# Storing the last group's expert results by tile and gathering them by token, with eight fours merged into the last attention

## Chip, core and metric

The kernel runs on one core of one Trainium2 chip. The metric is device time in microseconds (us) of one execution. Five engines work beside each other: PE (matrix multiplication), DVE (vector), ACT (scalar), POOL (GpSimd) and SP, which here only issues transfers. SP and ACT issue transfers with fixed addresses. POOL issues the indirect ones, whose row numbers stand in a tile. All transfers run on the same 16 DMA engines.

## What is computed

One decoder layer in float32 over 8 batches of 512 tokens and 256 features: a rolling attention, a cross attention with a causal mask, and a mixture of 16 routed experts, of which each token takes the best two, beside two shared ones.

```python
x = x + attn(layernorm(x), W_A, W_V, W_O, b_O)
x = x + xattn(layernorm(x), ctx, ctx, WK, WV, WQ)
flat = layernorm(x)
out = einsum(silu(flat @ wg_s) * (flat @ wu_s), wd_s)          # shared experts
probs = softmax(flat @ router_w)
weights, indices = top_k(probs, 2)                             # two experts a token
h = silu(flat @ wg_r[e]) * (flat @ wu_r[e]) * comb[e]
x = x + out + einsum(h, wd_r)                                  # routed experts
```

## The kernel before

The batches are worked one after another. Batch b runs its attentions while the next batch's first part and the last batch's shared experts are merged in, in an order written out by hand (`ORDER`, `ORDER6`, `ORDER7`). A framework (Tile) then takes the instructions, places the waits, hands out the buffers, and orders each engine's queue by a planner with its own estimates of durations. Within its queue an engine works strictly in order. A tile's tag names a small set of buffers (`bufs`); a new tile of that tag waits until everything that read an old one is done.

**Routed experts.** The batches form two groups (`GROUPS`): batches 0 to 6, and batch 7 alone. `ranked` (L567 on) counts for each token where it stands in the list of each of its two experts. `send` (L606) then writes the normalised row, with the token's number and weight, to that place in the DRAM tensor `xg` of the group, by one indirect transfer for 128 rows. `tiled` (L661 on) works out how the 16 lists fall into tiles of 128 rows: `begin` is the first tile of an expert, `n` its count of rows. The first group has 72 tiles, the second 24. Four tiles make a "four" (`QT = 4`), so there are 18 and 6 fours.

For each four `fetch` (L736) loads the rows, `pick` (L745, L755) the weights of the experts, `turn` (L763 to L776) transposes the rows, `hidden` (L790 to L794) and `down` (L805 to L819) compute, and `put` (L827) writes each of the four result tiles to the DRAM tensor `yg` by token: an indirect transfer on POOL whose row numbers (`to`) come with the rows. Rows that fill up a tile have a number beyond the bound, and are dropped. The result tiles `y` lie in buffers of the tag `y` (eight tiles, two fours) or `xT` (four buffers of one four each, which other tiles use too: the normalised rows `x2T` of batch 7 hold one of them until the shared experts of batch 7 are done).

**The end.** `MIXED` is the number of the first group's fours that are merged step by step into the last attention; the fours from there on are merged with the ranking, the sending and the tiling of batch 7 (`sorting`). The six fours of the second group follow, merged with the shared experts of batch 7 (`late`, L632 to L651). `take` (L879) loads what was put for one batch, two times 512 KB, on SP; `join` (L890) adds both to `x` on DVE, and L892 stores the batch. The takes of a batch use one of three pairs of buffers, by the batch's number modulo 3: `qT` for batches 0, 3 and 6, `v2` for 1, 4 and 7, `row` for 2 and 5. A take of the first group waits for all 72 puts of that group; the take of batch 7 for all 24 of its own.

Of the kernel before, what the change touches and what calls it, by code (L numbers as in the profile page):

```python
# [16 lines left out]
P = 128  # L17
B, S, D = 8, 512, 256
NT = S // P
KC = D // P  # L20
H, HD = 16, 16
NE = 16
# [4 lines left out]

GROUPS = ((0, 1, 2, 3, 4, 5, 6), (7,))

MIXED = 5  # L30

STAY = (4, 5, 6, 7)

# [2 lines left out]
QT = 4  # L36


def n_tiles(g):

    n = (len(GROUPS[g]) * S * 2 + NE * (P - 1)) // P
    return -(-n // QT) * QT
# [43 lines left out]
def decoder_layer(ctx: ExitStack, tc: tile.TileContext, x, ctxT, waT, wvT, woT, bo, wkT, xwv, wqT, wr, wg, wu, wd, out):  # L86
    nc = tc.nc

    const = ctx.enter_context(tc.tile_pool(name="const", bufs=1))
    sb = ctx.enter_context(tc.tile_pool(name="sb", bufs=2))  # L90
# [4 lines left out]
    st = [dict() for _ in range(B)]  # L95
# [99 lines left out]
    grp = []  # L195
    for g, bs in enumerate(GROUPS):
        n = len(bs) * S
        first = const.tile([P, NE], F32, name=f"first{g}")
        nc.vector.tensor_scalar(first, expert_no, float(n + P), float(P), ALU.mult, ALU.add)


        xg = dram.tile([NE * (n + P) + P, XW], F32, tag=f"xg{g}", bufs=1, name=f"xg{g}")
        grp.append({
            "g": g, "n": n, "first": first, "xg": xg,
            "yg": dram.tile([2 * n, D], F32, tag=f"yg{g}", bufs=1, name=f"yg{g}"),
        })


# [189 lines left out]
    def steps_back(b):  # L398
# [168 lines left out]
        def ranked():  # L567

            g, bi = where[b]
            G = grp[g]  # L570
            tt, red = nc.vector.tensor_tensor, nc.vector.tensor_reduce
            both = small.tile([P, NT, NE], F32, tag="both", bufs=1, name=f"both{b}")
            tt(both, s["oh"][0], s["oh"][1], ALU.add)
            pk = ps.tile([P, 2, NT, NE], F32, tag="tr", bufs=2, name=f"pk{b}")
            nc.tensor.matmul(pk[:, 0], before, both, start=True, stop=True)
            nc.tensor.matmul(pk[:, 1], ones, both, start=True, stop=True)
            run = small.tile([P, NT + 1, NE], F32, tag="run", bufs=2, name=f"run{b}")
            nc.vector.tensor_copy(run[:, 0], G["first"] if bi == 0 else G["run"][:, NT])
            for c in range(NT):
                tt(run[:, c + 1], run[:, c], pk[:, 1, c], ALU.add)  # L580
            G["run"] = run
            at = small.tile([P, NT, NE], F32, tag="at", bufs=1, name=f"at{b}")
            tt(at, pk[:, 0], run[:, :NT], ALU.add)
            place = small.tile([P, 2, NT], I32, tag="place", bufs=2, name=f"place{b}")
            for r in range(2):
                hit = small.tile([P, NT, NE], F32, tag="hit", bufs=2, name=f"hit{b}_{r}")
                tt(hit, s["oh"][r], at, ALU.mult)
                spot = small.tile([P, NT], F32, tag="spot", bufs=2, name=f"spot{b}_{r}")
                red(spot, hit, AX.X, ALU.add)
                behind = nc.vector.tensor_copy(place[:, r], spot).ins  # L590
                with tc.issue_after(behind):
                    nc.vector.tensor_scalar_add(s["row"][r][:, :, 0], tok[:, bi * NT:(bi + 1) * NT], float(r * G["n"]))
            s["place"] = place
# [67 lines left out]
    def tiled(g):  # L661

        G = grp[g]
        T = n_tiles(g)
        tt = nc.vector.tensor_tensor

        def new(n, shape=(P, NE), dt=F32):
            return small.tile(list(shape), dt, tag=n, bufs=1, name=f"{n}_{g}")

        def per_tile(n, of, dt=F32):  # L670
            w, out = new("held"), new(n, (P, 1), dt)
            tt(w, here, of, ALU.mult)
# [24 lines left out]
        fit = new("fit")  # L697
        nc.vector.scalar_tensor_tensor(fit, G["run"][:, NT], -float(P), row, ALU.add, ALU.min)
        last = new("last", (P, 1))
        nc.vector.tensor_reduce(last, here, AX.X, ALU.add)  # L700
        nc.vector.tensor_scalar(last, last, -float(NE * (G["n"] + P)), float(NE * (G["n"] + P)), ALU.mult, ALU.add)
        row0 = per_tile("row0", fit)
        tt(row0, row0, last, ALU.add)
        G["table"] = row0, ex

        tt(row, row, fit, ALU.subtract)
        G["had"] = per_tile("had", row)

    def tabled(g):

# [15 lines left out]
    def steps_routed(g):  # L726
# [32 lines left out]
        def turn(q):  # L759
            def f():  # L760
                xs = G["xs", q]
                G["to", q] = small.tile([P, QT], I32, tag="to", bufs=8, name=f"to{g}_{q}")
                nc.vector.tensor_tensor(G["to", q], xs[:, :, 0], G["far"][:, q * QT:(q + 1) * QT], ALU.max)  # L763

                G["w", q] = small.tile([P, QT], F32, tag="w", bufs=8, name=f"w{g}_{q}")
                nc.vector.tensor_copy(G["w", q], xs[:, :, 1])
                xT = sb.tile([P, KC, QT, P], F32, tag="xsT", name=f"xsT{g}_{q}")
                for k in range(KC):
                    pt = ps.tile([P, 512], F32, tag="tr", bufs=2, name=f"pxt{g}_{q}_{k}")
                    for i in range(QT):  # L770
                        nc.tensor.transpose(pt[:, i * P:(i + 1) * P], xs[:, i, 2 + k * P:2 + (k + 1) * P], ident)  # L771
                    to = xT[:, k].rearrange("p i t -> p (i t)")
                    if k == 0:
                        nc.scalar.copy(to, pt)
                    else:
                        nc.vector.tensor_copy(to, pt)  # L776
                G["xT", q] = xT
            return f
# [19 lines left out]
        def down(q):  # L798
            def f():
                h, wdn = G["h", q], G["wdn", q]  # L800
                tag = "mm" if g or q >= MIXED else "gu"
                py = [ps.tile([P, QT // 2, D], F32, tag=tag, bufs=3, name=f"py{g}_{q}_{o}") for o in range(2)]
                for j in range(QT // 2):
                    for o in range(2):
                        nc.tensor.matmul(py[o][:, j, :], h[o * MR:(o + 1) * MR, j, :], wdn[o * MR:(o + 1) * MR, j, :], start=True, stop=True)  # L805
                if g == 0 and (q < MIXED or q % 2 == 0):
                    y = [sb.tile([P, D], F32, tag="y", bufs=8, name=f"y{g}_{q}_{i}") for i in range(QT)]
                else:

                    y = sb.tile([P, QT, D], F32, tag="xT", bufs=4, name=f"y{g}_{q}")  # L810
                    y = [y[:, i, :] for i in range(QT)]
                for o in range(2):
                    for j in range(QT // 2):
                        i = 2 * j + o
                        w = G["w", q][:, i:i + 1]
                        if j == 0:
                            nc.scalar.mul(y[i], py[o][:, j, :], w)  # L817
                        else:
                            nc.vector.tensor_scalar_mul(y[i], py[o][:, j, :], w)  # L819
                G["y", q] = y  # L820
            return f

        def put(q, n):
            def f():
                o, j = divmod(n, 2)
                i = 2 * j + o
                ins = nc.gpsimd.indirect_dma_start(  # L827
# [9 lines left out]
                tc.add_to_no_dep_group(f"take{g}", ins)  # L837
                G["put_ins"] = ins
            return f

        nq = n_tiles(g) // QT
        first = [lambda: tiled(g), lambda: tabled(g), *[fetch(q) for q in range(3)], pick(0), turn(0)]
# [108 lines left out]
    late = list(shared[B - 1].values())  # L951
    last = backs[B - 1]

    sorting = [last["rk"], first1[0], first1[1]]
    for i in range(8):
        sorting += [last[f"sd{i}"], *idle(1)]

# [7 lines left out]
    for f in tail:  # L965
# [7 lines left out]
        while done < len(joins) and ("h_ins", min(done + 4, n_tiles(1) // QT - 1)) in grp[1]:  # L973
# [1 line left out]
            if done + 3 < len(takes):  # L975
                takes[done + 3]()
            done += 1
    keeps, takes, joins = steps_join(1)
    for f in [*takes, *joins]:
        f()  # L980


# ---- launch: one core; the host only lays data out
# [51 lines left out]
```

## Time and profile before

| | |
|---|---|
| Median of 3 runs | 613.17 us (612.73 to 613.65) |
| The profiled execution | 565.26 us, its span 563.4 us |
| Busy: PE, DVE, POOL, ACT | 508.4, 369.3, 229.7, 190.8 us |
| Mean granted PE clock | 0.955 |
| Puts on POOL (L827) | 96, 1.031 us each |
| Sends on POOL (L606) | 64, 0.986 us each |
| Joins on DVE (L890) | 16, 1.22 us each |

The profile is of one execution, and its times run from the first instruction (0) to the last (563.4). "Busy" sums what an engine executes; the issue of a transfer is not in it. In a row of the timeline the first number is the start, the second the time to the end of the piece, then engine, source line and operation, then output and inputs by their names; the brackets give idle time before it and what ended it. In a table of windows each engine has its busy time, with the number of instructions in brackets; then come the granted PE clock, the mean busy share of the 16 DMA engines, and their rate in GB/s. The profiled execution is 48 us shorter than the runs, so differences are worked out within the profile.

### The profile page before, as it was taken

How to read it: one execution, taken by the hardware profiler on the slowest of the kernel's cores; microseconds unless marked ns; L12 is line 12 of the kernel's file. 1: busy time of each engine (PE TensorE's matmuls, PEld its weight loads, DVE VectorE, ACT ScalarE, POOL GpSimd, SP SyncE). 2: the span in 40 equal slices, each digit the busy share in tenths (PEclk: the TensorE clock that was granted, in tenths of full speed). 3: DMA queues.
4: the chain of work that ended last, by engine and by line, in shares of the span. 5: the costliest groups of instructions: out<-in, count | busy, mean ns of one | idle time of the engine just before them, and what ended most of it. 6: DMA issues, size and time to landing. Idle time of an engine off the chain costs nothing.

```text
span 563.4 us, 10081 instructions
## 1 busy us (share of the span) xinstructions
PE 508.4 (90%) x3172; PEld 337.5 (60%) x3172; DVE 369.3 (66%) x1290; ACT 190.8 (34%) x483; POOL 229.7 (41%) x257
## 2 busy tenths in 40 slices
PE   7989989999999999999999999998988898898750
PEld 5546625666675765766666656556655786687320
DVE  4448757768777876866876874885447464444682
ACT  2233313322333224233222333124544376653110
POOL 2400502530640523343144061150547577777880
PEclk9999999999999999999999999999988799988695
DMA  8880280671392175058156138216746578975996
GB/s 269 267 336 4 71 313 9 196 293 68 116 350 99 59 276 224 35 198 316 52 178 227 38 109 307 94 48 170 216 133 210 170 232 261 279 233 191 301 322 223
DMA packets 63532, 105.57 MB, mean 187 GB/s; under 512 B 8839, under 2 KB 37518, under 8 KB 63378
## 3 DMA queue, kind: packets, MB, share of 16 engines
q1 hardware_dynamic: 48216, 79.68, 42.6%
q0 software_dynamic: 7680, 16.87, 8.1%
q10 hardware_dynamic: 7584, 8.39, 4.7%
q8 instruction: 25, 0.41, 0.3%
q14 instruction: 27, 0.22, 0.1%
HBM read 81.30 MB, written 33.33 MB: 203 GB/s over the span
## 4 chain that ended last, share of the span: by engine, by line
PE 56%; DMA 13%; DVE 13%; POOL 5%; issue 4%; SPq 4%; ACT 2%; POOLq 0%; ACTq 0%; DVEq 0%
PE pc L411 8%; DMA yg<-y,to 5%; PE pv L379 5%; PE psc L463 4%; PE pa L492 4%; PE pd L649 4%; PE pt L269 4%; PE pq L367 4%; PE po L445 3%; PE pv L351 3%; PE pgu L790 3%; PE pu L632 3%; PE pg L632 3%; PE pxt L771 3%; DMA T<-zd 2%
## 5 line engine op out<-in xcount | busy, mean ns | idle before, releaser
L253 POOL TENSOR_TENSOR rs<-ve,power 128x2 f32<-128x2 f32 x48 | 35.2, 740 | 204.2 <-DVE ve L252 202.3
L827 POOL DMA_INDIRECT yg<-y,to x96 | 99.0, 1031 | 45.7 <-ACT y L817 19.1
L606 POOL DMA_INDIRECT xg<-row,place x64 | 63.1, 986 | 31.5 <-issue 17.3
L411 PE MATMUL pc<-T,vh 128*32 128x256 f32 (+1 forms) x512 | 60.6, 500 | 2.2 <-DMA T<-zd 1.2
L790 PE MATMUL pgu<-xsT,wgu 128*64 128x128 f32 x768 | 52.5, 286 | 0.9 <-DVE r L557 0.5
L790 PEld LDWEIGHTS pgu<-xsT,wgu 128*64 128x64 f32 x768 | 44.4, 142 | 7.5 <-issue 6.1
L805 PE MATMUL py<-wdn,rh 64*128 64x256 f32 x192 | 38.5, 448 | 5.3 <-DVE y L819 5.2
L463 PE MATMUL psc<-kT,qT 128*128 128x128 f32 (+3 forms) x128 | 40.2, 439 | 1.2 <-DVE kT L274 1.2
L238 DVE BATCH_NORM_STATS2 bn<-x 128x6 f32<-128x256 f32 x96 | 38.0, 412 | 4.2 <-DMA x<-in_x_dram 3.2
L411 PEld LDWEIGHTS pc<-T,vh 128*32 128x32 f32 x512 | 20.7, 110 | 32.2 <-issue 19.3
L492 PE MATMUL pa<-v,pT 128*128 128x256 f32 x160 | 40.0, 381 | 0.0
L771 PE MATMUL pxt<-ident,xs 128*128 128x128 f32 x192 | 32.5, 304 | 7.4 <-DMA xs<-xg 5.4
L649 PE MATMUL pd<-wd_sb,h 128*128 128x256 f32 x128 | 34.0, 386 | 2.7 <-DVE h L636 2.6
L492 PEld LDWEIGHTS pa<-v,pT 128*128 128x128 f32 x160 | 29.4, 190 | 10.9 <-issue 3.7
L819 DVE TENSOR_SCALAR y<-py,w 128x256 f32<-128x256 f32 x48 | 22.1, 479 | 20.3 <-ACT y L817 20.0
L745 ACT COPY wgu<-wgu_r 128x256 f32 x96 | 33.4, 403 | 3.4 <-DVE pT L483 1.9
L351 PE MATMUL pv<-wv_sb,xr 128*128 128x272 f32 (+1 forms) x128 | 31.9, 394 | 2.7 <-ACT xr L344 2.7
L771 PEld LDWEIGHTS pxt<-ident,xs 128*128 128x128 f32 x192 | 23.2, 153 | 17.5 <-DMA xs<-xg 7.3
L257 DVE TENSOR_SCALAR xn<-x,mv,rs 128x256 f32<-128x256 f32 x64 | 28.1, 478 | 8.4 <-POOL rs L253 7.5
L632 PE MATMUL pg<-x2T,wg_sb 128*128 128x512 f32 x64 | 33.0, 619 | 0.0
L817 ACT ACTIVATE y<-py,w 128x256 f32<-128x256 f32 x48 | 21.7, 470 | 31.7 <-DMA yg<-y,to 19.3
L805 PEld LDWEIGHTS py<-wdn,rh 64*128 64x128 f32 x192 | 22.1, 205 | 15.8 <-DVE y L819 7.1
(172 smaller groups left out, 933.5 us busy)
## 6 DMA issues: line engine op xcount, KB each, us to landing
T<-zd SPq DMA_DIRECT2D x32, 1024.0 KB
xs<-xg SPq DMA_DIRECT2D x96, 129.0 KB
yj<-yg SPq DMA_DIRECT2D x16, 512.0 KB
x<-in_x_dram SPq DMA_DIRECT2D x8, 512.0 KB
ctxT<-in_ctxT_dram SPq DMA_DIRECT2D x8, 512.0 KB
xg<-blank SPq DMA_DIRECT2D x6, 516.0 KB
wdn<-wdn_d ACTq DMA_DIRECT2D x48, 64.0 KB
wdn<-wdn_d SPq DMA_DIRECT2D x48, 64.0 KB
```

Source lines behind the costliest of these rows:

```text
L238: nc.vector.bn_stats(stats["bn"][:, c, :], src[:, c, :])
L351: nc.tensor.matmul(pv[:, :w], xr[:, k, i, :], wv_sb[:, k, :w], start=(k == 0), stop=(k == KC - 1))
L411: nc.tensor.matmul(s["pc"][o][32 * g:32 * g + 32, 2 * jp * P:], vh[:, jp, h, :], s["T"][h // HPT][:, h % HPT, :S - 2 * jp * P], start=(jp ...
L463: nc.tensor.matmul(pc[:, :w], s["qT"][:, k, i * P:w], s["kT"][:, k, :w], start=(k == 0), stop=(k == KC - 1))
L492: nc.tensor.matmul(pa[:, :D], s["pT", i][:, j * P:(j + 1) * P], s["v2"][:, j, :], start=(j == 0), stop=(j == i))
L606: ins = nc.gpsimd.indirect_dma_start(out=grp[g]["xg"][:, :], out_offset=bass.IndirectOffsetOnAxis(ap=s["place"][:, r, c:c + 1], axis=0), i ...
L632: nc.tensor.matmul(p, w[:, k, mt * P:(mt + 1) * P], s["x2T"][:, k, :], start=(k == 0), stop=(k == KC - 1))
L649: nc.tensor.matmul(pd[:, i, :], s["h", mt][:, c * P:(c + 1) * P], wd_sb[:, mt, :], start=(mt == 0), stop=(mt == NSH - 1))
L771: nc.tensor.transpose(pt[:, i * P:(i + 1) * P], xs[:, i, 2 + k * P:2 + (k + 1) * P], ident)
L790: nc.tensor.matmul(p[o * MR:(o + 1) * MR, n, j, :], wgu[:, i, n, k, :], xT[:, k, i, :], start=(k == 0), stop=(k == KC - 1))
L805: nc.tensor.matmul(py[o][:, j, :], h[o * MR:(o + 1) * MR, j, :], wdn[o * MR:(o + 1) * MR, j, :], start=True, stop=True)
L827: ins = nc.gpsimd.indirect_dma_start(out=G["yg"][:, :], out_offset=bass.IndirectOffsetOnAxis(ap=G["to", q][:, i:i + 1], axis=0), in_=G["y" ...
```

## The change

For the second group, `put` issues nothing for single tiles. Once a four is complete, one transfer from ACT stores its four tiles as they are, in the order of the tiles, to `yg` (which grows to 24 times 128 rows). A new step `found` works out on DVE, for each token and each of its two experts, the row of `yg` at which its result lies: the place in the expert's list, moved by `begin` of the expert; an expert's last tile is counted back from its end, so a row beyond it is shifted. After everything else eight indirect transfers on POOL gather these rows, for each of the four tiles of tokens one for either expert, into two tiles of the tag `qT`. Two adds and a store on SP follow for each tile of tokens. The take and the join of batch 7 are gone. `MIXED` goes from 5 to 8, which also changes where the results of fours 5 to 7 are kept: the tag `gu` in place of `mm` in PSUM, and `y` in place of `xT` for fours 5 and 7.

```diff
-MIXED = 5
+MIXED = 8
...
-            "yg": dram.tile([2 * n, D], F32, ...),
+            "yg": dram.tile([2 * n if g == 0 else n_tiles(g) * P, D], F32, ...),
...
+    def found(b):
...
+        tt(k, s["at"], wide(G["first"]), ALU.subtract)
+        nc.vector.tensor_copy(ki, k)
+        nc.vector.tensor_single_scalar(ki, ki, 7, ALU.logical_shift_right)
+        nc.vector.tensor_copy(u, ki)
+        nc.vector.tensor_scalar(u, u, float(P), float(P), ALU.mult, ALU.add)
+        tt(u, u, wide(G["count"]), ALU.subtract)
+        nc.vector.scalar_tensor_tensor(u, u, 0.0, k, ALU.max, ALU.add)
+        nc.vector.scalar_tensor_tensor(u, wide(G["begin"]), float(P), u, ALU.mult, ALU.add)
+        s["found"] = small.tile([P, 2, NT], I32, tag="place", ...)
+        for r in range(2):
+            tt(hit, s["oh"][r], u, ALU.mult)
+            nc.vector.tensor_reduce(spot, hit, AX.X, ALU.add)
+            nc.vector.tensor_copy(s["found"][:, r], spot)
...
         def turn(q):
-                G["to", q] = ...
+                if g == 0:
+                    G["to", q] = ...
...
         def put(q, n):
+                if g == 1:
+                    if n == 1:
+                        store(q)
+                    return
...
+        def store(q):
+            nc.scalar.dma_start(out=G["yg"][q * QT * P:(q + 1) * QT * P, :].rearrange("(i p) d -> p i d", p=P), in_=G["y4", q])
...
-    sorting = [last["rk"], first1[0], first1[1]]
+    sorting = [last["rk"], first1[0], first1[1], lambda: found(B - 1)]
...
-    keeps, takes, joins = steps_join(1)
-    for f in [*takes, *joins]:
-        f()
+    x = st[B - 1]["x"]
+    y = [sb.tile([P, NT, D], F32, tag="qT", bufs=2, name=f"yl{r}") for r in range(2)]
+    for c in range(NT):
+        for r in range(2):
+            nc.gpsimd.indirect_dma_start(
+                out=y[r][:, c, :],
+                out_offset=None,
+                in_=grp[1]["yg"][:, :],
+                in_offset=bass.IndirectOffsetOnAxis(ap=st[B - 1]["found"][:, r, c:c + 1], axis=0),
+            )
+        for r in range(2):
+            nc.vector.tensor_tensor(x[:, c, :], x[:, c, :], y[r][:, c, :], ALU.add)
+        nc.sync.dma_start(out=out[B - 1, c * P:(c + 1) * P], in_=x[:, c, :])
```

More of the change, by code (lines that the diff above doesn't have):

```diff
@@ L204, in decoder_layer @@
             "g": g, "n": n, "first": first, "xg": xg,
-            "yg": dram.tile([2 * n, D], F32, tag=f"yg{g}", bufs=1, name=f"yg{g}"),
+            "yg": dram.tile([2 * n if g == 0 else n_tiles(g) * P, D], F32, tag=f"yg{g}", bufs=1, name=f"yg{g}"),
         })
@@ L583, in ranked @@
             tt(at, pk[:, 0], run[:, :NT], ALU.add)
+            s["at"] = at
             place = small.tile([P, 2, NT], I32, tag="place", bufs=2, name=f"place{b}")
@@ L704, in tiled, with new, wide @@
         G["table"] = row0, ex
+        G["begin"], G["count"] = begin, n
         tt(row, row, fit, ALU.subtract)
         G["had"] = per_tile("had", row)
+    def found(b):
+        g, bi = where[b]
+        G, s = grp[g], st[b]
+        tt = nc.vector.tensor_tensor
+        def new(n, dt=F32):
+            return small.tile([P, NT, NE], dt, tag=n, bufs=1, name=f"f{n}_{b}")
+        def wide(t):
+            return t.unsqueeze(1).to_broadcast([P, NT, NE])
+        k, ki, u = new("r2"), new("r3", I32), new("r6")
+        tt(k, s["at"], wide(G["first"]), ALU.subtract)
[6 more added lines that the diff above has]
+        nc.vector.scalar_tensor_tensor(u, wide(G["begin"]), float(P), u, ALU.mult, ALU.add)
+        s["found"] = small.tile([P, 2, NT], I32, tag="place", bufs=2, name=f"found{b}")
+        for r in range(2):
+            hit = small.tile([P, NT, NE], F32, tag="hit", bufs=2, name=f"fhit{b}_{r}")
+            tt(hit, s["oh"][r], u, ALU.mult)
+            spot = small.tile([P, NT], F32, tag="spot", bufs=2, name=f"fspot{b}_{r}")
+            nc.vector.tensor_reduce(spot, hit, AX.X, ALU.add)
+            nc.vector.tensor_copy(s["found"][:, r], spot)
     def tabled(g):
@@ L761, in f @@
                 xs = G["xs", q]
-                G["to", q] = small.tile([P, QT], I32, tag="to", bufs=8, name=f"to{g}_{q}")
-                nc.vector.tensor_tensor(G["to", q], xs[:, :, 0], G["far"][:, q * QT:(q + 1) * QT], ALU.max)
+                if g == 0:
+                    G["to", q] = small.tile([P, QT], I32, tag="to", bufs=8, name=f"to{g}_{q}")
+                    nc.vector.tensor_tensor(G["to", q], xs[:, :, 0], G["far"][:, q * QT:(q + 1) * QT], ALU.max)
                 G["w", q] = small.tile([P, QT], F32, tag="w", bufs=8, name=f"w{g}_{q}")
@@ L810, in f @@
                     y = sb.tile([P, QT, D], F32, tag="xT", bufs=4, name=f"y{g}_{q}")
+                    G["y4", q] = y
                     y = [y[:, i, :] for i in range(QT)]
```

## Prediction

> **What bounds the kernel now.** The change touches only what follows the last attention's start, so I read the page's list of groups first, then a table of windows over that part, then the timelines of POOL, DVE and SP, and the waits.
>
> ```profile
> L827 POOL DMA_INDIRECT yg<-y,to x96 | 99.0, 1031 | 45.7 <-ACT y L817 19.1
> ```
>
> This group is POOL's 96 puts. The windows, with the columns described above:
>
> ```profile
> 395.80:451.00 55.20, 47.38 (x402) 35.11 (x402) 29.87 (x124) 24.60 (x66) 31.77 (x33) 0.85 0.61 180
> 451.00:513.60 62.60, 58.63 (x656) 46.04 (x652) 31.77 (x91) 37.88 (x99) 47.73 (x49) 0.97 0.79 237
> 514.70:551.50 36.80, 23.50 (x86) 13.13 (x86) 25.35 (x33) 6.89 (x17) 27.77 (x24) 0.80 0.93 315
> 517.90:524.40 6.50, 4.69 (x34) 3.64 (x34) 1.98 (x3) 0.12 (x2) 5.28 (x5) 0.50 1.03 392
> 551.50:563.40 11.90, 0.00 (x0) 0.00 (x0) 2.45 (x2) 0.00 (x0) 0.00 (x0) 0.50 0.58 197
> ```
>
> Three stages are to be seen. From 451 to 513.6 POOL issues 49 indirect transfers in 62.6 us, one every 1.28 us: 0.97 us of work and 0.30 us between, without a break. PE, 94% busy there, runs ahead until it lacks result buffers; the first group's last put goes out 19 us after its last matmuls (PE ends them at 493.5). From 395.8 to 451 POOL issues only 33 in 55.2 us, which is where it loses time. From 514.7 the DMA engines are 93% busy: the loads for the first group's joins cannot begin before its last put has landed. The last window is a chain with one thing at a time. POOL's timeline, cut to the rows I use:
>
> ```profile
> 512.62 0.97 POOL L827 DMA_INDIRECT yg<-y,to  x1 [0.30 <-issue]
> ...
> 519.00 1.88 POOL L827 DMA_INDIRECT yg<-y,to  x1 [0.30 <-issue]
> ...
> 548.20 1.28 POOL L827 DMA_INDIRECT yg<-y,to  x1 [0.30 <-issue]
> ```
>
> The put at 512.62 is the first group's last (24 follow); the one at 548.20 ends the second group. The timelines of SP and DVE:
>
> ```profile
> 514.70 3.19 SPq L879 DMA_DIRECT2D yj<-yg  x6
> 531.59 22.48 SPq L879 DMA_DIRECT2D yj<-yg  x8
> ...
> 518.82 1.22 DVE L890 TENSOR_TENSOR xj<-xj,yj 128x1024 f32<-128x1024 f32 x1
> 524.87 0.48 DVE L819 TENSOR_SCALAR y<-py,w 128x256 f32<-128x256 f32 x1 [4.84 <-ACT y L817]
> 525.27 1.22 DVE L890 TENSOR_TENSOR xj<-xj,yj 128x1024 f32<-128x1024 f32 x1
> ...
> 550.26 1.23 DVE L890 TENSOR_TENSOR x<-x,yj 128x1024 f32<-128x1024 f32 x1 [0.49 <-DMA yj<-yg]
> 557.12 2.53 DVE L890 TENSOR_TENSOR x<-x,yj 128x1024 f32<-128x1024 f32 x2 [5.63 <-DMA yj<-yg]
> ```
>
> The joins start at 518.8, but DVE, in order, stands 4.84 us behind a result of the second group, and again 3.6 us before 537.16. The reason is in the waits from 440 us on: ACT's evacuations wait for puts to land and free a buffer.
>
> ```profile
> ACT y L817 <- DMA yg<-y,to: 19.3, 4, 6.4
> ```
>
> Batch 6 is joined by 551.5. Then the last takes, two adds and the store of batch 7 need 11.9 us to the end at 563.4.
>
> **The change part by part.** I sum three terms: A, when the first group's last put lands (514.7 now); B, from there to the end of batch 6's join (36.8 us now); C, from there to the end (11.9 us now).
>
> *A: eight fours in the attention.* From its first put in the attention (395.83) to 513.6 POOL has 117.8 us. It issues 72 puts and 8 sends, 80 x 1.28 = 102.4 us, and about 2 us of small operations (two powers of 0.74, a copy of 0.61). 13.4 us are idle, nearly all before 451: POOL starves while PE works attention steps and then waits for the ranking and tiling of batch 7. Three fours more lie between those steps. Of the 13.4 us I take back 6: the chain of ranking and tiling (DVE small operations from 428 to 440, PE only 1.76 us busy in 436 to 440, its clock then 0.50) is moved later, not removed. Bounds: 11 us, if only the start-up gaps stay; 0 or 3 us worse, if the y tag, which now carries fours 5 and 7 too and holds two fours, makes PE wait for POOL inside the attention, where POOL's two powers queue behind puts and DVE stands behind them. The sends follow later by the three fours, but 20 puts (25.6 us) still lie behind the last of them, and the send's landing and the loads took 15 us before (475.5 to 490.9). `found` adds 14 DVE operations of 0.15 to 0.23 us, 2.6 us, where DVE is busy 14.80 of 25 us (425 to 450); without that cover it costs at most 2.6. Sums in gu instead of mm, and six `to` operations of 0.16 us fewer, I cost at nothing: fours 0 to 4 run so already, and PE has POOL's lag to hide in. A = -6.
>
> *B: stores for scatters.* Gone are 24 puts, POOL's work from 513.89 to 549.48, and with them ACT's 19.3 us of waiting: a store frees its buffer by itself. DVE's two stands, 4.8 and 3.6 us, go. Late next is the DMA traffic. The 24 puts move at most 1024 real rows, 1.05 MB; six stores write all 3.15 MB, about four of them after the takes begin, so 2.1 MB beside 7.34 MB of takes and some 2.6 MB of output before batch 6 is loaded: 12.0 MB. At the 315 GB/s of the third window this takes 38 us, at the 392 GB/s of the fourth, where loads were queued without a hole, 30.7. The Trainium skill, "DMA: Bandwidth & Descriptors", Specifications, gives about 358 GB/s as a core's HBM limit; that would make 33.5 us. The trace holds 392 for 6.5 us, so 358 is no ceiling here; but holes will remain, since a take needs the buffers of the join three before it. I take 33.5 from between my two rows, so B = -3.3 (bounds -6 and +1.5). The six store issues go into ACT's queue (about 0.4 us each, 2.4 in all). Each waits for DVE's half of its four; behind it stand the next weight copies and tanh. At most 0.9 us each, 5 us, of a PE chain that would end near 525 to 530 with the shared experts of batch 7, while batch 6 is joined at 542. So nothing, and without that cover 5.
>
> *C: the gathers.* The new tiles take the tag qT, whose last user is batch 6. The take of batch 7 used v2, which batch 4 left. So no gather starts before batch 6's adds are over: the first buffer 1.2 us before the end, the second at the end. Then POOL issues eight. Beside a join a put took 1.88 us and not 0.97, so the first gather costs about 1.9, and six small adds beside the others (a half tile of 128x512 takes 0.69 us on DVE, so 128x256 about 0.35) stretch them by some 1.8 together. Counted from the end of batch 6's adds, POOL is done at -1.2 + 1.9 + 0.3 + 7 x 1.28 - 0.3 + 1.8 = 11.5. No gather is in the trace; the nearest row is a put that landed in 2.05 us on quiet engines (the last one, into traffic, 4.98). With 2.2 for landing, 0.4 for the last add, 0.4 for the store's issue, and 3.3 from there to the end (now 560.1, the last store issued, to 563.4): 11.5 + 2.2 + 0.4 + 0.4 + 3.3 = 17.8. The three earlier tiles' stores overlap, and without the stretching it is 16. I take 17: C = +5.1, bounds +3 and +8.
>
> Sum: -6 - 3.3 + 5.1 = -4.2. The profiled execution goes from 565.26 to 561.1. The median is 48 us longer for a reason that the profile doesn't show; I carry the difference over as it is: 613.17 - 4.2 = 609.0.
>
> **The rivals.** *The gathers become the bound (slower).* The new wait, gathers behind batch 6's buffers, with eight issues in a row on an idle chip, takes the place of the puts. It decides as soon as A and B together bring less than C's 5.1 us. For it: DMA is 93% busy already and gets 1.05 MB more after the takes begin, and POOL's gaps before 451 may come from the ranking, which stays. With A = -1, B = +1.2 (38 us against 36.8) and C = +5.1 the sum is +5.3: 618.5. Against it: the 19.3 us of waiting that surely go. Chance 0.40 for all that is slower by over 0.2%.
>
> *POOL packed and DMA without holes.* A = -11, B = -6, C = +4: -13, 600.2. For it: the 35.6 us of POOL taken out behind 513.89, and 392 GB/s shown. Against it: PE was 94% busy from 451 to 513.6, so it cannot supply fours much faster than POOL drains them. Chance 0.14.
>
> *The eight fours do nothing.* A = 0, the same starving only moved: -3.3 + 5.1 = +1.8, 615.0. It lies in the slower share.
>
> *A draw*, within 0.2% (1.2 us, about what a measurement of this kernel can tell from no change): 0.10.
>
> **How the numbers follow.** My own forecast, about -1.2 to -9 us, has 0.36, and with the larger gain 0.50 is faster, 0.10 the same, 0.40 slower. Its own range is 604 to 612. The range for 8 in 10 runs from 600.5, near the large gain, to 619.5, just above the slower rival; a tenth lies beyond either end.
>
> **What would show it.** A: POOL's 72nd put of the first group, and with it SP's first L879 row, near 508.7 and not 514.7, and more than 33 issues in the 55 us from the first put of the attention. B: no wait of ACT's L817 on yg in the last 60 us; joins following each other, the last of batch 6 ending near 542; DMA rate from the takes on near 360 GB/s. C: eight indirect transfers on POOL in one row after that, some 11 us, starting within a microsecond of batch 6's adds; span end 17 us after them. It would be wrong if the takes start no earlier, if batch 6's join ends later than 546 (then the gathers make it slower), or if PE waits for the y tag inside the attention.

## The result, and the profile after

The changed kernel takes 618.92 us (median of 5 runs, 617.57 to 620.03), and the kernel before took 613.17 beside it (612.73 to 614.99): a ratio of 1.0087, with an interval of 1.0064 to 1.011. It is 5.75 us slower where 4.2 us of gain were forecast.

One thing has to be known to read what follows. How long the kernel before takes depends on the job, a series of runs on one chip: 613 and 619 us in two jobs, 562 to 563 us in four others on four other chips. I call the two kinds the 615-us and the 562-us chips, though each job ran on one chip, so that chip and job can't be told apart. The execution that the prediction was read from (565.26 us) is of the second kind, and the runs that were to be predicted are of the first. Every ratio here is against the kernel before in the same job. Executions over 1.5% longer than the fastest of their kernel are left out of the ratios but not of the medians, so the two can differ a little.

The profile after (span 617.3 us, of a 615-us chip) has therefore to be set against a profile of the kernel before from such a chip: `a_before`, the unchanged kernel once more, span 616.2 us. It comes from the other job of that kind, where the kernel before takes 619.4 us and not 613.2: the two spans differ by 1.1 us where the medians of one job differ by 5.75, and what lies ahead of the first take (562.30 and 569.31) can't be compared between them. `c_after5` below is a partner from the same job. First the groups of the page of after, the line that answers to that of L827:

```profile
L865 POOL DMA_INDIRECT yg<-y,to x72 | 70.4, 978 | 72.6 <-ACT y L851 51.6
```

POOL has 24 puts fewer. But it waited 51.6 us for results of ACT (19.1 in the line shown before): in this stretch POOL is not what holds the others up. The windows of after, with B and C as the third and fourth, and then those of `a_before`, cut at the same events:

```profile
396.00:450.00 54.00, 42.03 (x374) 30.27 (x372) 21.93 (x69) 21.19 (x58) 28.81 (x30) 0.94 0.58 175
450.00:547.90 97.90, 72.86 (x482) 51.03 (x484) 33.87 (x134) 32.58 (x83) 50.65 (x52) 0.67 0.44 137
562.30:597.35 35.05, 20.90 (x120) 10.92 (x117) 23.62 (x32) 8.78 (x23) 0.00 (x0) 0.80 1.02 365
597.35:617.30 19.95, 6.10 (x14) 4.45 (x14) 5.75 (x12) 0.00 (x0) 7.86 (x8) 0.59 0.46 148
```

```profile
453.00:548.70 95.70, 69.87 (x542) 50.49 (x542) 27.52 (x77) 32.54 (x88) 51.62 (x53) 0.77 0.49 147
569.31:609.02 39.71, 26.12 (x166) 16.15 (x162) 27.33 (x40) 8.98 (x22) 23.07 (x20) 0.93 0.90 302
609.02:616.20 7.18, 0.00 (x0) 0.00 (x0) 2.45 (x2) 0.00 (x0) 0.00 (x0) 0.50 0.76 279
```

B (first take to the end of batch 6's join) went from 39.7 to 35.1 us, C (from there to the end) from 7.2 to 20.0. And between 450 and 548 POOL issues 52 indirect transfers in 98 us, where the execution read before had 49 in 62.6: the packed POOL of step A isn't there.

SP's timeline of `a_before` shows what the first take really stood behind on this chip, and POOL's its last put of the first group:

```profile
562.95 4.39 SPq L736 DMA_DIRECT2D xs<-xg  x4
568.07 1.14 SPq L755 DMA_DIRECT2D wdn<-wdn_d  x2
569.31 5.61 SPq L879 DMA_DIRECT2D yj<-yg  x5
```

```profile
547.71 0.98 POOL L827 DMA_INDIRECT yg<-y,to  x1 [0.30 <-issue]
```

The last put was issued at 547.71, the first take at 569.31, 21.6 us after the put was issued. In between SP issues the rows and weights of the second group's fours, with no hole above 1.2 us from 552.8 on, and the takes stand behind them in its queue. In the execution read before, SP was through with those ahead of the takes at 509.80 and stood idle until the put had landed, at 514.70.

The last stage of after, on DVE, ACT and POOL:

```profile
594.48 1.22 DVE L931 TENSOR_TENSOR x<-x,yj 128x1024 f32<-128x1024 f32 x1
595.61 0.48 DVE L853 TENSOR_SCALAR y<-py,w 128x256 f32<-128x256 f32 x1
596.12 1.23 DVE L931 TENSOR_TENSOR x<-x,yj 128x1024 f32<-128x1024 f32 x1
...
614.20 0.42 DVE L1031 TENSOR_TENSOR x<-x,yl 128x256 f32<-128x256 f32 x1 [0.37 <-DMA yl<-yg,found]
```

```profile
596.12 0.37 ACTq L880 DMA_DIRECT2D yg<-y  x1
```

```profile
602.35 1.00 POOL L1024 DMA_INDIRECT yl<-yg,found  x1 [54.43 <-PE pd L651]
603.65 0.96 POOL L1024 DMA_INDIRECT yl<-yg,found  x1 [0.30 <-issue]
...
611.40 0.95 POOL L1024 DMA_INDIRECT yl<-yg,found  x1 [0.30 <-issue]
```

The last four's result (L853 at 595.61) stands on DVE between the two adds of batch 6's join. So its store is issued at 596.12, and the first gather starts at 602.35, 6.2 us after that and 5.0 us after the join's end at 597.35. There are eight gathers, 1.24 to 1.48 us apart. In `a_before` nothing of this is there: its last put is issued at 599.03, 10 us before batch 6 is joined, and batch 7's first add follows 0.5 us after batch 6's last.

### The profile page after: what moved, and what is told of

Read it like the earlier page. It is cut to its first block, busy times and chain, and to the rows that moved or that the text cites. A ratio compares the mean times of both kernels' runs of the same rounds, so it can differ in the third digit from the quotient of the medians.

```text
span 617.3 us, 10040 instructions
## 1 busy us (share of the span) xinstructions
PE 534.4 (87%) x3172; PEld 352.0 (57%) x3172; DVE 370.4 (60%) x1304; ACT 190.8 (31%) x483; POOL 209.1 (34%) x241
## 4 chain that ended last, share of the span: by engine, by line
PE 59%; DVE 11%; DMA 9%; another core or an unknown queue 6%; issue 5%; POOL 4%; ACT 2%; SPq 2%; ACTq 1%; POOLq 0%; DVEq 0%
PE pc L412 7%; PE py L838 5%; PE pv L380 4%; PE pgu L823 4%; PE psc L464 4%; PE pa L493 4%; PE pv L352 4%; PE pt L270 4%; PE pd L651 3%; PE pq L368 3%; PE pxt L804 3%; PE po L446 3%; PE pu L634 3%; PE pg L634 3%
## 5 line engine op out<-in xcount | busy, mean ns | idle before, releaser
L865 POOL DMA_INDIRECT yg<-y,to x72 | 70.4, 978 | 72.6 <-ACT y L851 51.6
L823 PE MATMUL pgu<-xsT,wgu 128*64 128x128 f32 x768 | 66.2, 304 | 19.9 <-issue 12.5
L823 PEld LDWEIGHTS pgu<-xsT,wgu 128*64 128x64 f32 x768 | 50.5, 152 | 33.5 <-issue 26.0
L838 PE MATMUL py<-wdn,rh 64*128 64x256 f32 x192 | 42.3, 468 | 9.9 <-DVE rh L827 3.9
L809 DVE COPY xsT<-pxt 128x512 f32<-128x512 f32 x24 | 16.5, 688 | 42.1 <-remote 20.5
L651 PE MATMUL pd<-wd_sb,h 128*128 128x256 f32 x128 | 37.1, 416 | 5.1 <-DVE h L638 3.7
L804 PE MATMUL pxt<-ident,xs 128*128 128x128 f32 x192 | 36.1, 327 | 5.8 <-ACT xsT L807 2.2
L634 PE MATMUL pu<-x2T,wu_sb 128*128 128x512 f32 x64 | 33.2, 626 | 5.5 <-DVE h L638 5.5
L838 PEld LDWEIGHTS py<-wdn,rh 64*128 64x128 f32 x192 | 24.0, 216 | 21.9 <-issue 10.6
L804 PEld LDWEIGHTS pxt<-ident,xs 128*128 128x128 f32 x192 | 26.0, 167 | 17.9 <-issue 8.4
L853 DVE TENSOR_SCALAR y<-py,w 128x256 f32<-128x256 f32 x48 | 22.9, 480 | 15.6 <-issue 9.1
```

The lines of the kernel that those rows point to most:

```text
L634: nc.tensor.matmul(p, w[:, k, mt * P:(mt + 1) * P], s["x2T"][:, k, :], start=(k == 0), stop=(k == KC - 1))
L651: nc.tensor.matmul(pd[:, i, :], s["h", mt][:, c * P:(c + 1) * P], wd_sb[:, mt, :], start=(mt == 0), stop=(mt == NSH - 1))
L823: nc.tensor.matmul(p[o * MR:(o + 1) * MR, n, j, :], wgu[:, i, n, k, :], xT[:, k, i, :], start=(k == 0), stop=(k == KC - 1))
L865: ins = nc.gpsimd.indirect_dma_start(out=G["yg"][:, :], out_offset=bass.IndirectOffsetOnAxis(ap=G["to", q][:, i:i + 1], axis=0), in_=G["y" ...
```

## The experiments

**The parts by themselves, on a 615-us chip** (before: 619.4 us). `a_before` is the unchanged kernel.

> The kernel before, unchanged, to see an execution of its ordinary length: the prediction was read from one of 565 us, the runs take 613. Theory 'slow issue': the ordinary profile has a span near 611, some 48 us longer than the 563 that I read, and all of it lies between the last attention (about 395) and the first L879 take, in stretches in which PE, DVE and SP issue one instruction in 0.7 to 1.3 us, as the changed kernel's profile shows from 440 to 550; the takes then start near 562 and not at 514.7, and from there to the end it is 49 us as before. Rival 'launch': the 48 us lie outside the span or evenly over it; takes start at 514.7 plus less than 10.

618.52 us, 1.0005 (0.9982 to 1.0029): two medians of one kernel agree to about 0.2%. The first take lies at 569.31, 54.6 us later than in the execution read before, and from there to the end it is 46.9 us against 48.7. So all of the extra time lies ahead of the first take, as the first theory said.

`b_mixed8` is the kernel before with eight fours in the attention and nothing else:

```diff
-MIXED = 5
+MIXED = 8
```

> The kernel before with MIXED = 8 alone. Theory 'gathers': the eight fours are not the cost, 611 to 613.5 (0 to -2 us), and the change's +5.75 lies in the end. Rival 'eight fours': the buffers of the y tag and the later ranking cost here, 616 to 620 (+3 to +6), the start of the takes moving by as much.

619.73 us, 0.9992 (0.997 to 1.0013): no difference. Its first take is at 569.70, where `a_before` has 569.31. Step A is nothing on this chip.

`c_after5` is the changed kernel with five fours, the gathers and stores alone:

```diff
-MIXED = 8
+MIXED = 5
```

> The changed kernel with MIXED = 5, so the stores and gathers alone. Theory 'gathers': 618 to 620 (+5 to +7), the end from the first take on about 55 us as in the changed kernel against 49. Rival 'eight fours': 610 to 614 (-3 to +1), since the end is then not what costs.

626.19 us, 1.0117 (1.0084 to 1.015): 6.8 us slower than before. In its profile B is 35.1 and C 19.9 us, against 39.7 and 7.2: -4.6 and +12.7, the same as in the whole change. Its first take is 0.9 us earlier than that of `a_before`, and the three sum to +7.2. The loss belongs to the gathers.

`d_v2` is the whole change with the gathered tiles in buffers that batch 4 has left, so that no gather waits for batch 6's:

```diff
-    y = [sb.tile([P, NT, D], F32, tag="qT", bufs=2, ...
+    y = [sb.tile([P, NT, D], F32, tag="v2", bufs=2, ...
```

> The changed kernel with the gathers' two tiles in the tag v2 (last read by batch 4's join) and not qT (batch 6's). Theory 'last store': in the changed kernel's trace the gathers start at 602.35, 5 us after batch 6's last add (597.35), when the last four's store, issued at 596.1 because its evacuation on DVE stands behind the joins, has landed; the tag then brings nothing, 618 to 620. Rival 'buffers': the gathers wait for qT as I predicted; with v2 they start near the join of batch 4 and 4 to 8 us go, 611 to 615.

620.9 us, 1.0033 (1.0013 to 1.0053). The first gather starts at 605.44, 5.2 us after the join's end at 600.26, as without the edit. The tag was not what the gathers wait for. The kernel comes out 5.3 us below `c_after5`, from which it differs by the eight fours and by the tag. C is the same in both profiles (20.1 and 19.9), and the first take is 2.4 us earlier in this one; so it looks as if the eight fours brought it, though alone they brought nothing here. The ratio is also below the 1.0087 of the change itself, which was not run in this job: whether the tag or the job makes that difference is not shown.

**The whole change on a 562-us chip** (before: 562.37 us). `e_after` is the changed kernel as it is.

> The changed kernel again, on the chip of the runs beside it, as their measure: 1.0087 of before as in its first runs (1.0064 to 1.011), the end from the first take to the last instruction near 55 us.

564.12 us, 1.0032 (1.0011 to 1.0053), where 1.0087 was expected. The profiled execution was one of 570.87 us, so that its absolute times say little; its C is 19.9 us, with the first gather 4.9 us after the join.

**The late store.** `f_evac` is the changed kernel with all tiles of the second group scaled by ACT, so that no store stands behind a join:

```diff
-                        if j == 0:
+                        if j == 0 or g == 1:
                             nc.scalar.mul(y[i], py[o][:, j, :], w)
```

> The changed kernel with all result tiles of the second group evacuated by ACT, none by DVE. Theory 'last store': the stores no longer stand behind the joins in DVE's queue; the last one is issued near the fifth evacuation, some 12 us before batch 6's last add, so the gathers start within 1 us of that add and not 5 after it: 4 us less than the changed kernel (ratio to before near 1.002). Rival 'buffers alone' (the gathers wait for something else that lies at the end, such as the shared experts): no gain, 1.0087.

561.03 us, 0.9974 (0.9951 to 0.9997), 3.1 us below `e_after`. Its ACT and POOL rows:

```profile
527.72 0.62 ACTq L880 DMA_DIRECT2D yg<-y  x1
```

```profile
541.23 1.25 POOL L1024 DMA_INDIRECT yl<-yg,found  x1 [36.98 <-PE pd L651]
...
550.31 0.95 POOL L1024 DMA_INDIRECT yl<-yg,found  x1 [0.30 <-issue]
```

The last store is issued 13.9 us before the join's end at 541.61, and the first gather starts 0.4 us before that end instead of 4.9 after it. C is 15.1 us. So the late store cost 4.8 us of the last stage (19.9 in `e_after` and in `n_after5` below). The medians show 3.1 of them; B is 1.9 us longer than in the profile of `e_after` (35.8 and 33.9). The same kernel twice more:

> The changed kernel, with all four tiles of the second group's fours scaled by ACT, so that the last four's store does not stand behind the joins on DVE. An earlier run of the same kernel gave 0.9974 of the kernel before where that took 562.4 us. Theory 1 (the late store is what the end pays): its first gather starts within 1 us of the end of batch 6's join and not 5 us after it, and it is about 5 us faster than the changed kernel's 1.0087, so about 1.000 of the kernel before. Theory 2 (the gain came from elsewhere in that execution): 1.008, first gather again 5 us after the join.

559.88 us, 0.9966 (0.9949 to 0.9984), first gather at 546.38, 0.1 us after the join's end.

> As i_evac: the changed kernel with all four tiles of the second group's fours scaled by ACT; 0.9966 and 0.9974 where the kernel before took 562 us. If this job shows about 615 us: theory 1 (the late store costs 5 us in the end there too): 1.000, first gather within 1 us of batch 6's join. Theory 2 (the gain belongs to the quick chip alone): 1.008. At 562 us: 0.997.

562.82 us, 0.9986 (0.9958 to 1.0014), first gather 0.1 us after the join's end, on a 562-us chip again, so that the 615-us chip stays untried. `j_bevac` is the control, the same edit on the kernel before:

> The kernel before with the same edit alone: ACT scales all four result tiles of each of the second group's fours, DVE none. Theory 1 (the edit is worth something only where a store waits for a whole four): no gain, 1.000, or up to 2 us slower, since ACT there also waits for landed puts. Theory 2 (relieving DVE is worth 3 us with or without gathers): 0.995.

560.74 us, 0.9981 (0.9959 to 1.0002): some 1.2 us of the gain could be had without gathers, which the interval doesn't tell from nothing.

**Gathers beside the joins.** `g_evac_xs` is `f_evac` with the gathered tiles in the tag `xs`, free long before:

> As the last one, and the gathers' tiles lie in the tag xs, whose last reader is the second group's transposition. Theory 'last store and buffers': nothing of the end holds the gathers any more; they run beside the joins once the last store has landed (about 10 us before batch 6's last add), and the end after the joins shrinks from 20 us to 8 to 12, so 8 to 12 us less than the changed kernel, 0.990 to 0.996 of before. Rival 'traffic': beside takes at 400 GB/s the gathers land late and hold the joins up by as much; no more than 3 us come.

561.59 us, 0.9976 (0.9955 to 0.9997): nothing gained. The first gather still starts at the join's end (539.95 against 539.74), though the last store was issued at 527.93. `l_wide` goes on from there: the stores write 4 KB pieces (a partition's four rows next to each other), and eight more small DVE operations for each rank turn the row numbers.

```diff
-.rearrange("(i p) d -> p i d", p=P), in_=G["y4", q])
+.rearrange("(p i) d -> p i d", p=P), in_=G["y4", q])
```

> As i_evac, with the gathered tiles in the tag xs (free long before), and the six stores written so that a partition's four rows lie next to each other in yg: 4 KB pieces where the stores had 1 KB pieces, as the takes beside them have; nine small DVE operations for each expert rank turn the row numbers, 18 x 0.15 = 2.7 us, hidden. Theory 1 (the last store lands late because its 1 KB pieces get a small share of the DMA engines beside the takes' 4 KB pieces): it lands some 5 us after its issue, the first gather starts before batch 6's join ends, 4 to 7 us earlier, and the end follows: 0.990 of the kernel before. Theory 2 (the total of bytes decides, or the gather waits for something else): first gather at the end of batch 6's join as without it, 0.997 to 1.000.

560.39 us, 0.998 (0.9957 to 1.0003). The first gather is 2.7 us ahead of the join's end at 549.04, not 4 to 7, and C is 12.3 us; the time didn't follow (B is 36.8 us, where `g_evac_xs` has 35.1).

What holds the first gather can be read from the semaphore signals in the traces. Before it POOL's queue passes five to seven waits, one after the other. The traces record them; those of `after` (starts from 601.3 to 602.2), and the last five of `g_evac_xs`:

```profile
L1024 POOLq EVENT_SEMAPHORE  x6: 17/43/43, 601.3 to 602.2; - x6
```

```profile
L1024 POOLq EVENT_SEMAPHORE  x5: 17/43/43, 539.0 to 539.8; - x5
```

In every profile with gathers one of these waits ends within 0.03 us of the last of the 16 signals by which the last store of results reports its landing. The gather starts 0.90 to 1.05 us later, when the waits behind it have been passed:

| | last store issued | landed | first gather |
|---|---|---|---|
| `after` | 596.12 | 601.30 | 602.35 |
| `d_v2` | 599.00 | 604.39 | 605.44 |
| `f_evac` | 527.72 | 540.33 | 541.23 |
| `i_evac` | 533.00 | 545.48 | 546.38 |
| `g_evac_xs` | 527.93 | 538.96 | 539.95 |
| `l_wide` | 534.58 | 545.35 | 546.34 |

So the landing of the last store decides in all of them. PE's pd and the output's store, which the timelines name as releasers, belong to other waits of the same row and had signalled in time. With ACT's scaling the last store goes out 14 us before the join's end and not 1.2, but it takes 10.8 to 12.6 us to land and not 5.2 to 5.4, beside takes that keep the DMA engines full (`g_evac_xs`, from the store's issue to its landing):

```profile
527.90:539.00 11.10, 6.50 (x14) 4.27 (x15) 8.65 (x10) 0.00 (x0) 0.00 (x0) 0.54 1.05 404
```

That is why freeing the buffers gained nothing. Theory 1 of `l_wide` fails: 4 KB pieces land after 10.8 us, 1 KB pieces after 11.0 to 12.6. Theory 2, by which the total of bytes decides, fits, but what sets the landing time there is not shown.

**Without puts.** `h_noput`, `k_noput` and `o_noput` are one kernel in three jobs: each of the 96 puts of the kernel before is a plain transfer from ACT to fixed rows, which leaves out the order by token. It was to show on a 615-us chip whether the long stretch from 395 us on comes with POOL's indirect transfers, but all three fell on 562-us chips.

> The kernel before with every put on POOL replaced by a plain transfer of the same 128 x 256 tile from ACT, to fixed rows (the results are not brought into the order of the tokens; what is joined is therefore not the result). Theory 'puts slow the core': in the ordinary profile PE, DVE, ACT and SP go forward in steps of about 0.7 us while POOL's indirect transfers follow each other, and run freely where they don't; without them the stretch from 395 to the first take shrinks by 40 to 50 us and the kernel takes 560 to 580. Rival 'something else' (loads with row numbers from registers, small packets, the clock): 605 to 620, ACT's 96 issues adding a little.

> The kernel before with each of its 96 puts replaced by a plain transfer of 128 rows from ACT to fixed rows, so the result rows lie in the order of the tiles and are added to the wrong tokens; 12.6 MB are written where the puts write 8.4. Where the kernel before took 562.4 us this took 579.7. If the job shows about 562 us for the kernel before, again 1.03. If it shows about 615 us: theory 1 (the slow stretch from 395 us on comes with POOL's indirect transfers, so it goes when 96 of them go): about 580 us, 0.94. Theory 2 (the slow stretch has nothing to do with them): the 17 us come on top, about 632 us, 1.03.

> As k_noput: each put of the kernel before replaced by a plain transfer of 128 rows from ACT to fixed rows (rows are added to the wrong tokens). Where the kernel before took 562 us this took 577 to 580. If this job shows about 615 us for the kernel before: theory 1 (the slow stretch from 395 us on comes with POOL's indirect transfers): about 580 us, 0.94. Theory 2 (it has nothing to do with them): about 632 us, 1.03. If the job shows 562 us again it gives 1.03 and says nothing new.

579.7, 577.06 and 579.6 us: 1.0311, 1.0278 and 1.0297. There it is 15 to 18 us slower, and the question isn't touched.

**Eight fours and five, on 562-us chips.** `m_mixed8` is `b_mixed8` again, `n_after5` is `c_after5` again.

> The kernel before with MIXED = 8 alone, as in an earlier run that gave 0.9992 where the kernel before took 619.4 us. There POOL was not the bound ahead of the first take. If this job shows about 562 us for the kernel before, POOL is packed there (an issue every 1.28 us), as in the execution that the forecast was read from. Theory 1 (step A holds where POOL is the bound): first take about 6 us earlier, 0.990. Theory 2 (PE is the bound of that stretch too, and POOL's lag hides in it): 1.000.

555.03 us, 0.9872 (0.9832 to 0.9912): 6.8 us faster than before (561.86). Its POOL and SP rows, and the last two windows:

```profile
505.44 0.97 POOL L827 DMA_INDIRECT yg<-y,to  x1 [0.30 <-DVE w L766]
```

```profile
508.48 3.25 SPq L879 DMA_DIRECT2D yj<-yg  x6
```

```profile
508.48:543.41 34.93, 22.86 (x130) 13.68 (x128) 26.49 (x37) 6.69 (x16) 27.39 (x23) 0.88 0.97 336
543.41:555.70 12.29, 0.00 (x0) 0.00 (x0) 2.45 (x3) 0.00 (x0) 0.00 (x0) 0.50 0.53 183
```

The first group's last put is at 505.44 and not 512.62, the first take at 508.48 and not 514.70. Step A had said 508.7. But single executions differ by as much: `j_bevac`, which has five fours, has its first take at 508.66 in an execution of 558.92 us, and the two other profiles with eight fours and puts have 504.84 and 506.28. The size of the step stands on the medians.

> The changed kernel with MIXED = 5, as in an earlier run that gave 1.0117 where the kernel before took 619.4 us; there its first gather came 5 us after the join and its last stage took 19.9 us. Theory 1 (eight fours are worth nothing, gathers and stores make the whole difference): the same as the changed kernel on the same kind of chip, 1.003 at 562 us or 1.009 at 615. Theory 2 (eight fours are worth some 5 us once the puts behind them are gone): 1.010 at 562 us or 1.012 and more at 615.

567.18 us, 1.0099 (1.0066 to 1.0131): 5.3 us slower. Its last two windows:

```profile
511.76:545.75 33.99, 20.08 (x106) 11.29 (x102) 23.33 (x31) 7.12 (x17) 0.00 (x0) 0.77 0.96 344
545.75:565.60 19.85, 5.46 (x14) 4.00 (x14) 5.76 (x12) 0.00 (x0) 7.85 (x8) 0.59 0.51 164
```

Against the windows of before that the prediction shows, B is 2.8 us shorter and C 8.0 us longer: +5.2, which is what the medians say.

**The version that came out best.** `r_mixed8` is eight fours alone once more, `q_mix8ev` eight fours with ACT's scaling.

> The kernel before with MIXED = 8 alone, once more. It gave 0.9872 where the kernel before took 562 us and 0.9992 where it took 619 us. Theory 1 (eight fours are worth the 6 us of step A where POOL issues without a break ahead of the first take, and nothing elsewhere): again 0.987 at 562 us, with the first take 6 us earlier than 514.7; or 1.000 at 615. Theory 2 (the 0.9872 was a good draw of six runs): 0.995 at 562 us.

557.36 us, 0.9899 (0.9862 to 0.9936).

> The kernel before with MIXED = 8, and ACT scaling all four tiles of the second group's fours (0.9981 alone). Theory 1 (the two edits relieve different stretches, one ahead of the first take, one behind it): 0.985 at 562 us. Theory 2 (ACT then stands longer behind puts that have not landed): 0.990, slower than eight fours alone.

557.28 us, 0.9894 (0.9863 to 0.9925): the second edit adds nothing to the first. Eight fours without gathers beat both kernels on the 562-us chips, and neither help nor hurt on the 615-us one.

## Why the prediction was wrong, point by point

The parts, as differences of medians from the kernel before of the same job:

| | 562-us chips | 615-us chips |
|---|---|---|
| eight fours alone | -6.8, -5.9 us | +0.3 us |
| gathers and stores alone | +5.3 us | +6.8 us |
| both | +1.8 us | +5.75 us; with the other tag +1.5 us |

**Step C failed most: it was mis-sized.** It said +5.1. The pair of profiles from 615-us chips shows +12.8 (7.2 to 20.0), the pair from 562-us chips +8.0 (11.9 to 19.9). Of 12.8 - 5.1 = 7.7 us, 3.0 are the new end, 20.0 instead of 17.0. I let the first gather start with batch 6's adds, 1.2 us before their end, because its buffers come free there. It starts 5.0 us after them: the last four's result stands in DVE's queue between those very adds, so its store is issued 1.2 us before their end, needs 5.2 us to land, and POOL's waits take 1.0 more. `f_evac` shows this term (4.8 us of C gone when the result leaves DVE), `d_v2` that the buffers I had named don't decide, and the table of landings what does. I had written that each store waits for DVE's half of its four, and looked only at what is queued behind it on ACT, not at who waits for the store; its landing has no term in the sum. The rest of the stage ran shorter than I had it: from the first gather to the end 617.3 - 602.35 = 15.0 us, where an end at 17 and a first gather at -1.2 made 18.2. The eight gathers took 10.0 us and not 12.7, since the stretching that I had put in didn't come (the longest took 1.17 us).

The other 4.7 us lie in the 11.9 that I subtracted. That row holds batch 7's take waiting for its puts, whose last was issued at 548.20: the take goes out at 553.23, 1.7 us after the end of batch 6's join. In `a_before` the last put is 10 us ahead of that end, the take 5.2 us (603.81), and batch 7's first add waits 0.5 us. But 7.2 is the old end of one execution. In `b_mixed8`, from the same job and with the same end, the take goes out 1.7 us ahead (608.24), and C is 10.6:

```profile
609.93:620.57 10.64, 0.00 (x0) 0.00 (x0) 2.45 (x3) 0.00 (x0) 0.00 (x0) 0.50 0.71 204
```

So on the 615-us chips C lost something between 9.3 and 12.8 us: the 3.0 us of the new end are firm, and of the old end 1.3 to 4.7 us.

**Step A failed by being carried over.** Its size is right where I read it: -6 was said, and the medians of eight fours alone show -6.8 and -5.9 (`m_mixed8`, `r_mixed8`). That the first take of `m_mixed8` agrees to 0.2 us (508.48, said 508.7) is luck, as the other profiles show. On the timed kind of chip the step alone is nothing (`b_mixed8`): the takes there stand in SP's queue behind the loads of the second group's fours, and POOL's last put has been issued long before (552.73, first take 569.70). The prediction named the 48 us between profile and median and carried them over as an offset that leaves every step alone. They are no offset: they lie ahead of the first take (514.70 there, 569.31 in `a_before`), and change what that take waits for. The rival "eight fours do nothing" (615.0) is what happened to this step alone.

**Step B came out.** -3.3 was said; -4.7 on the timed kind (39.7 to 35.1), -2.8 on the other. The rate was to be near 360 GB/s, and is 365 and 344. What ACT waited for puts is gone. In the waits of after (ACT, from 440 us on) a wait for another landing stands in its place, 5.4 us at the store issued at 577.55, for which I had given 5 us as the price without cover; that it cost anything is not shown:

```profile
ACT y L851 <- DMA yj<-yg: 5.4, 1, 5.4
```

One part of B's reasoning was wrong without a cost that is seen: PE's chain was to end 12 us and more before batch 6's join, and in `after` it ends at 604.1, 6.8 us behind it. The adds of the shared experts that it feeds come at 601.82 and 608.01; the first is over before the first gather has landed, and the second waits for nothing.

**The sum.** The single parts don't quite add. On the 562-us chips they give -6.8 + 5.3 = -1.5 us (-0.6 with the other run), and both together show +1.8: some 3 us of what eight fours bring would be lost when the gathers are there. The parts come from three jobs with intervals of 1 to 2 us each, so this is hardly clear of noise. On the 615-us chip it is the other way about: eight fours bring nothing alone, and up to 5.3 us beside the gathers (`c_after5` to `d_v2`, which differ by the tag too). Why is open. The slower rival gave 618.5, which the median meets by luck and not by its own terms: it had B = +1.2 and C = +5.1, and the runs show B below zero and C at +9 to +13.

What stays open as well is why one chip needs 50 us more. In the stretch from 400 to 550 us its PE goes ahead by single matmuls. Two pieces of PE's timeline of `a_before`, and a put of the second group:

```profile
483.90 0.27 PE L790 MATMUL pgu<-xsT,wgu 128*64 128x128 f32 x1 [1.18 <-issue]
485.33 0.37 PE L790 MATMUL pgu<-xsT,wgu 128*64 128x128 f32 x1 [1.16 <-issue]
...
561.57 1.97 PE L790 MATMUL pgu<-xsT,wgu 128*64 128x128 f32 x32
```

```profile
561.40 0.97 POOL L827 DMA_INDIRECT yg<-y,to  x1 [12.72 <-ACT y L817]
```

At 561.57, 32 such matmuls take 1.97 us; at 484 they come one by one, 1.4 us apart, and the view can name no releaser ("issue"). The slow stretch lies beside POOL's transfers. But the 32 matmuls at 561.57 run beside puts too (from 561.40 on), so the transfers alone don't make it slow, and its cause isn't shown.

## What to carry to other kernels

When a profile is 8% shorter than the runs that it stands for, find out where the missing time lies before using any wait of it: a step that shortens a wait is worth nothing where that wait doesn't end last. For an operation moved to the end of a kernel, follow every producer back through its engine's queue, not only the buffers: here a result of 0.48 us that stood between two joins put off eight gathers by 5 us. Count such a store to its landing and not to its issue: issued 12.7 us earlier, beside full DMA engines, it landed only 5 us earlier. And parts of a change belong apart: eight fours alone gained 6 us on one kind of chip and cost nothing on the other, and the gathers that came with them lost it.

## What the runs showed of the hardware

The same program takes about 562 or 615 us according to the job, each on one chip, with nearly the same spread within each (558.29 to 566.43 over 59 runs, 614.43 to 624.57 over 59). On the 615-us chip the extra time lies all ahead of the first take (54.6 us between `a_before` and the execution read before), and single matmuls come 1.4 us apart in part of that stretch of `a_before`; the granted clock is 0.67 in after's window from 450 on. A gather of 128 rows costs POOL the same as a put, 0.95 us and 0.30 between, and its add follows 2.8 us after its issue starts (602.35 to 605.16). A store of 512 KB from ACT landed 5.2 us after its issue in `after`, where the last take had landed by then (596.03), and 10.8 to 12.6 us after it where takes were still under way (`f_evac`, `i_evac`, `g_evac_xs`, `l_wide`; 404 GB/s in `g_evac_xs`). The windows of B hold 365 GB/s for 35 us in after and 375 in `f_evac`, above the 358 that the Trainium skill, "DMA: Bandwidth & Descriptors", lists under Specifications as a core's HBM limit, and under Measured ties to both cores of an HBM domain streaming; this kernel runs on one core, and the measurement decides.
